# Attention in pairs of heads: scores of two pairs in one group, exponentials a beat late, two key buffers, values loaded pair by pair

## The chip, the cores and the metric

The kernel runs on one NeuronCore of a Trainium2 chip. The metric is the device time of one execution in microseconds (us), the median of several runs. Before the change it is 1545.6 us (three runs, 1545.55 to 1545.87).

Five engines work side by side, each through its own instructions in order: TensorE (PE; its weight loads appear as PEld), VectorE (DVE), ScalarE (ACT), GpSimd (POOL) and SyncE (SP), whose only work here is to issue transfers. Engines wait for one another through semaphores; what waits holds up everything behind it on its engine.

## The reference, cut to what matters

```
x = x + tanh(g_xattn) * attention(layernorm(x), ctx, mask, bias)     # 32 sequences of 64 tokens, width 512
x = x + tanh(g_ffn)   * lora_linear(layernorm(x))

def attention(hq, hkv, mask, bias):          # 32 heads of 128
    q, k, v = hq @ Wq, hkv @ Wk, hkv @ Wv
    score = q k^T / sqrt(128) + bias         # 64 x 64 for each sequence and head
    probs = where(mask, softmax(where(mask, score, -inf)), 0)
    return concat(probs @ v) @ Wo
```

Everything is float32. Most products are computed as three products of a high and a low part (a type of reduced precision, fp32r); scores and output products (probs @ v) are plain float32, which TensorE records as two passes each.

## The kernel before, in words

The 2048 tokens are worked off in two phases (`NPH`) of 1024. A phase first projects keys and values (`stage_a`) and stores them in HBM as `kd` and `vd`, then runs attention (`attention`, `run`) over 16 pairs of heads (`NPR`), and adds each pair's share of the output projection to an accumulator `acc`. The linear layer (`ffn_chunk`) follows the second phase.

The projections use seven products instead of eight for each block (`unit`, line 351): products called p1, p6, p7, p5, p2, p4, p3, in this order, each six matmuls of 512 columns. The weight of a pair is prepared by `pair_blocks` and `prep` (lines 267 to 313): four sums and seven high/low splits of 128 x 256, the high parts on ACT (L294), sums and low parts on the engine given, POOL or DVE (L287, L298). p6 needs the sums s3 and s2, in this order.

The order on each engine is that in which the Python code issues instructions (`manual_schedule`). Side work stands in generators in the list `streams`; `beat()` (line 64), called after each product, lets each of them issue one step, and `drain` issues all that is left. So the place of a step is counted in beats, of 1.36 us where a beat follows six matmuls.

For pair n the loop of `run` (lines 847 to 900) issues:

- the query unit: `unit(wq, xq)`, five of seven products, then the last two row tiles of the output projection of pair n-2 (`oproj`, L839 by way of `mm3`, L97), then the last two products (`end`);
- `pv(n-1)` (L812): 16 output products of 128 x 128 (L818, result `po`), copied to `ch` (ACT, L821) and its rest `cl` (DVE, L822);
- `scores(n, i)` for i = 0, 1 (L755): each 16 matmuls of 64 x 64, two at a time in halves of the array (L760, `ps`), then scale and bias (DVE, L762), row maximum (DVE, L764), subtraction (POOL, L765), exponential (ACT, L766);
- transfers: the next keys into one buffer `kB` (`load_k`, L702), the bias of the next pair into `sm`, and on even pairs the values of two pairs, 2 MB in two transfers (`load_v`, L706);
- six row tiles of `oproj(n-1)`. Beside them `softmax` (L769) issues by beats: sums and reciprocals (DVE), scaling (POOL), the turn `tp` (DVE), and 16 copies of 32 x 256 into `pt` (ACT, L793).

Pair 0 has a form of its own (`alone`): half of the turned probabilities are written by DVE in small transposes. The weight of pair 1 is prepared by DVE, that of pair 2 and later by POOL. At the end of a phase `last` does `finish` (two tiles of oproj(14)), other work (a half of the next phase's first key projection, or the first quarter of the linear layer), `attend` (`pv(15)`), and oproj(15).

Transfers go through SP's queue in order; each uses one of eight semaphores in turn, so a transfer is issued when the one eight places before it has landed.

Of the kernel before, what the change touches and what calls it, by code (L numbers as in the profile page):

```python
# [17 lines left out]
P = 128  # L18
# [25 lines left out]
def flamingo_block(ctx: ExitStack, tc: tile.TileContext, x, ctxT, bias, mask, gx, gf,  # L44
# [24 lines left out]
    def drain(g):  # L69
        if g in streams:  # L70
            streams.remove(g)
            for _ in g:
                pass
# [625 lines left out]
    def attention(p, res, rest):  # L699
        b = {}  # L700

        def load_k(n):  # L702
            b["k", n] = big(res[1], [P, 2, TP], F32, f"kB{p}_{n}")
            nc.sync.dma_start(out=b["k", n], in_=kd[p][n])

        def load_v(q):  # L706
            b["v", q] = [big(res[2 + c], [P, 4, 512], F32, f"v{p}_{q}_{c}") for c in range(2)]
            for c in range(2):
                nc.sync.dma_start(out=b["v", q][c], in_=vd[p][q][:, c * 4:(c + 1) * 4, :])
# [5 lines left out]
        def bias_mask(n):  # L715
            yield
            yield
            for i in range(2):
                yield
                t = sm[n % 2][:, i]  # L720
                nc.gpsimd.tensor_tensor(t, t, masks[p][0], ALU.add)  # L721

# [5 lines left out]
        def enter():  # L728
            nonlocal pt, sm
            if not sm:  # L730
                sm = [rwp.tile([P, 2, NT, S], F32, tag=f"r{2 + i}", name=f"sm{p}_{i}") for i in range(2)]
                load_bias(0)
                return bias_add
            if not pt:
                pt = big(res[0], [P, 2, NT, P], F32, f"pt{p}")
                nc.vector.memset(pt, 0.0)
                return
            fetch("q", p * NPR + 1, "r0")
            load_k(0)
            load_v(0)  # L740
# [14 lines left out]
        def scores(n, i, qT, kT):  # L755
# [9 lines left out]
            nc.gpsimd.tensor_tensor(s, s, mx.unsqueeze(2).to_broadcast([P, NT, S]), ALU.subtract)  # L765
            nc.scalar.activation(s, s, AF.Exp)  # L766
            beat()

        def softmax(n, pace):  # L769
            ss = [sm[n % 2][:, i] for i in range(2)]  # L770
            alone = pace is None
            tp = []

            def turn(i):
                tp.append(rows.tile([P, NT, S], F32, tag="row", name=f"tp{p}_{n}_{i}"))
                nc.vector.transpose(tp[i].rearrange("p a b -> p (a b)"), ss[i].rearrange("p a b -> p (a b)"))  # L776

            for i in range(2):
                nm = f"{p}_{n}_{i}"
                r = st.tile([P, NT], F32, tag="r", name=f"r{nm}")  # L780
                nc.vector.tensor_reduce(r, ss[i], AX.X, ALU.add)
                nc.vector.reciprocal(r, r)
                nc.vector.tensor_tensor(r, r, masks[p][1], ALU.mult)  # L783
                nc.gpsimd.tensor_tensor(ss[i], ss[i], r.unsqueeze(2).to_broadcast([P, NT, S]), ALU.mult)  # L784
                if alone and i:
                    turn(0)
                yield
            quads = [(h, qi, ki) for h in range(2) for qi in range(2) for ki in range(2)]

            def copy(f, i, of, h, qi, ki):  # L790
                src = slice(h * 64 + qi * 32, h * 64 + qi * 32 + 32)
                dst = slice(h * 64 + ki * 32, h * 64 + ki * 32 + 32)
                f(pt[dst, i, :, src], of[src, :, ki * 32:(ki + 1) * 32])  # L793

            if alone:
                for k, q in enumerate(quads):
                    copy(nc.scalar.copy, 0, tp[0], *q)
                    copy(nc.vector.transpose, 1, ss[1], *q)
                    if k % 3 == 2:
                        yield  # L800
                return
            for i in range(2):
                turn(i)
                yield
            todo = [(i, q) for i in range(2) for q in quads]
            for k in pace:
                for i, q in todo[:k]:
                    copy(nc.scalar.copy, i, tp[i], *q)
# [3 lines left out]
        def pv(n):  # L812

            for i, c in [(0, 0), (0, 1), (1, 0), (1, 1)] if n == 0 else [(0, 0), (1, 0), (0, 1), (1, 1)]:
                ps = psum(f"po{p}_{n}_{i}_{c}")
                hg = (2 * n + i) % 4
                for t in range(4):
                    nc.tensor.matmul(ps[:, t * P:(t + 1) * P], b["v", n // 2][c][:, t, hg * P:(hg + 1) * P],  # L818
                                     pt[:, i, c * 4 + t, :], start=True, stop=True)
                sl = slice(c * 512, (c + 1) * 512)  # L820
                nc.scalar.copy(ch[:, i, sl], ps)  # L821
                nc.vector.tensor_tensor(cl[:, i, sl], ps, ch[:, i, sl].bitcast(F32), ALU.subtract)  # L822
                beat()

        def prep_o(n):
            raw = raw_of.pop(("o", p * NPR + n))
            t = big(res[4], [P, 2, 1024], F32R, f"wo{p}_{n}")
# [8 lines left out]
        def oproj(n, t):  # L836
            w = b["o", n]
            ps = psum(f"pa{p}_{n}_{t}")
            sl = slice(t * P, (t + 1) * P)  # L839
            mm3(ps, [((ch[:, i, sl], cl[:, i, sl]), (w[:, 0, i * 512:(i + 1) * 512], w[:, 1, i * 512:(i + 1) * 512]))  # L840
                     for i in range(2)])
            nc.vector.tensor_tensor(acc[t], ps, acc[t], ALU.add)  # L842
            if n == NPR - 1 and p < NPH - 1:
                nc.sync.dma_start(out=x1d[t * P:(t + 1) * P, :], in_=acc[t])
            beat()

        def run(xq, prefetch, before_last, last_unit, last, between=None):
            soft = None
            for n in range(NPR):
                g = p * NPR + n  # L850
                qT = kqp.tile([P, 2, TP], F32, tag="kq", name=f"qT{g}")
                if n == 0:
                    qb = prep("q", g + 1, nc.vector, 2)
                    streams.append(qb)
                else:
                    streams.append(bias_mask(n))
                end = unit(wt[("q", g)], xq, None, k_dst(qT), f"q{g}", tuple(carry))
                carry.clear()
                if n == NPR - 1:
                    last_unit()  # L860
                if n == 1:
                    drain(qb)
                    fetch("q", g + 1, "r0")
                if n > 1:
                    oproj(n - 2, NT - 2)
                    oproj(n - 2, NT - 1)
                if n:
                    ob = prep_o(n - 1)
                    streams.append(ob)
                end()  # L870
                if n == 0:
                    enter_late()
                else:
                    drain(soft)
                if 0 < n < NPR - 1:
                    qb = prep("q", g + 1, nc.gpsimd, 2, 4)
                    streams.append(qb)
                if n:
                    pv(n - 1)
                    drain(ob)  # L880
                for i in range(2):
                    scores(n, i, qT, b["k", n])
                if n + 1 < NPR:
                    load_k(n + 1)
                    load_bias(n + 1)
                    if n % 2 == 0 and n:
                        load_v(n // 2)
                soft = softmax(n, None if n == 0 else (1, 2, 2, 3, 2, 2, 2, 2) if n < NPR - 1 or between else (4,) * 4)
                streams.append(soft)
                if n:  # L890
                    for t in range(NT - 2):
                        oproj(n - 1, t)
                        if n == NPR - 1 and between:
                            between(t)
                    drain(qb)
                    if n + 2 < NPR:
                        fetch("q", g + 2, "r0")
                    elif n + 2 == NPR:
                        before_last()
                if n == NPR - 5:  # L900
                    prefetch()
            ob = prep_o(n)

            def finish():
                oproj(n - 1, NT - 2)
                oproj(n - 1, NT - 1)
                streams.append(ob)

            def attend():
                drain(soft)  # L910
                drain(ob)
                pv(n)
            last(finish, attend, lambda t: oproj(n, t), acc)
# [7 lines left out]
    def frow(nm):  # L921
        rk[0] += 1
        return rwp.tile([P, 512], F32, tag=f"r{1 + rk[0] % 3}", name=nm)
# [115 lines left out]
    for p in range(NPH):  # L1039
# [4 lines left out]
        if p < NPH - 1:  # L1044
# [15 lines left out]
            def last(finish, attend, o, acc):  # L1060
                nonlocal more, kt0
                g = (p + 1) * NPR
                finish()
                fetch("k", g + 1, "r1")
# [4 lines left out]
                attend()  # L1069
# [5 lines left out]
            run(xq, prefetch, before_last, last_unit, last)  # L1075
        else:
# [11 lines left out]
            def last(finish, attend, o, acc):  # L1088
# [18 lines left out]
                finish()  # L1107
                drain(weights)
                ffn_chunk(0, first=False)
                attend()  # L1110
# [9 lines left out]
            run(xq, ffn_fetch, ffn_rows, last_unit, last, between)  # L1120
# [44 lines left out]
```

## Time and profile before

| what | value |
|---|---|
| median of the runs | 1545.6 us |
| profiled execution, its own time | 1545.82 us |
| its span, first to last instruction | 1543.8 us |
| TensorE busy | 1535.5 us (99%) |
| weight loads, VectorE, ScalarE, GpSimd busy | 1292.2, 948.3, 730.8, 1015.8 us |
| chain that ended last, share of TensorE | 95% |
| mean granted TensorE clock | 1.000 |

Lines of the profile read as follows. A group names line, engine, operation, output<-inputs, shapes and count, then the busy time in us, the mean length of one in ns, and the idle time of the engine before them with what ended it. The chain follows the work that ended last backwards; listed in order of time it gives start, length, and what. A timeline row gives start, length and count of merged instructions.

### The profile page before, as it was taken

To read this page: it belongs to the slowest core of one execution; us is meant where nothing else is said; L and a number is where in the kernel's file an instruction comes from. 1 tells how busy PE (TensorE), PEld (TensorE's weight loads), DVE (VectorE), ACT (ScalarE), POOL (GpSimd) and SP (SyncE) were. 2 spreads that over 40 slices of the span, in tenths; PEclk is the share of its full clock that TensorE was granted. 3 is DMA by queue.
4 is the path that set the end of the run, shared out by engine and by line. 5 is a ranking of instruction groups with operands and counts; after the bars stand their busy time and mean duration, and the time that the engine had idled before them with its cause. 6 is when DMAs were issued, how large, how long until landed. Compare 5 with 4: busy or idle time off the path is not lost.

```text
span 1543.8 us, 24975 instructions
## 1 busy us (share of the span) xinstructions
PE 1535.5 (99%) x9064; PEld 1292.2 (84%) x9064; DVE 948.3 (61%) x1579; ACT 730.8 (47%) x1610; POOL 1015.8 (66%) x1128
## 2 busy tenths in 40 slices
PE   9999999999999999999999999999999999999999
PEld 7888888888888888888888888888888888888887
DVE  5665343377676757575686535437767675757774
ACT  6454233345555555556445423334555555555621
POOL 3898378967665757575589837896766575757410
PEclk9999999999999999999999999999999999999999
DMA  5654444374243424531565544437424342444211
GB/s 207 243 191 177 165 171 164 137 280 177 83 177 136 163 87 177 190 141 67 213 222 191 178 170 166 164 136 282 176 83 178 137 158 94 174 189 147 80 42 69
DMA packets 80989, 246.37 MB, mean 160 GB/s; under 512 B 9857, under 2 KB 10881, under 8 KB 72674
## 3 DMA queue, kind: packets, MB, share of 16 engines
q1 hardware_dynamic: 80578, 244.26, 43.6%
q8 instruction: 71, 1.16, 0.3%
q10 hardware_dynamic: 288, 0.52, 0.1%
q14 instruction: 52, 0.43, 0.1%
HBM read 171.35 MB, written 73.40 MB: 159 GB/s over the span
## 4 chain that ended last, share of the span: by engine, by line
PE 95%; DMA 2%; DVE 2%; POOL 0%; issue 0%; ACT 0%; SPq 0%; DVEq 0%; POOLq 0%; ACTq 0%
PE pa L97 22%; PE po L818 7%; PE pzv L97 6%; PE pvv L97 6%; PE pxv L97 6%; PE pxq L97 5%; PE pzq L97 5%; PE pxk L97 5%; PE pzk L97 5%; PE pvk L97 5%; PE pvq L97 5%; PE ps L760 4%; PE ppk L97 3%; PE pyv L97 3%; PE pf L97 3%; PE pyk L97 2%
## 5 line engine op out<-in xcount | busy, mean ns | idle before, releaser
L97 PE MATMUL pa<-wo,ch 128*128 128x512 f32 x1024 | 319.9, 393 | 0.0
L793 ACT COPY pt<-tp 32x256 f32<-32x256 f32 x496 | 200.3, 404 | 87.7 <-DVE tp L776 76.6
L89 POOL TENSOR_TENSOR wo<-rawo,wo 128x512 fp32r<-128x512 f32 x64 | 81.1, 1286 | 223.3 <-ACT wo L88 215.5
L97 PEld LDWEIGHTS pa<-wo,ch 128*128 128x128 f32 x1024 | 189.4, 188 | 40.0
L842 DVE TENSOR_TENSOR acc<-pa,acc 128x512 f32<-128x512 f32 x256 | 170.0, 673 | 79.4 <-PE pa L97 79.3
L97 PE MATMUL pa<-wo,cl 128*128 128x512 f32 x512 | 199.7, 390 | 0.0
L818 PEld LDWEIGHTS po<-pt,v 128*128 128x128 f32 x1024 | 119.1, 192 | 2.6 <-ACT pt L793 0.2
L822 DVE TENSOR_TENSOR cl<-po,ch 128x512 fp32r<-128x512 f32 x128 | 88.3, 692 | 52.5 <-ACT ch L821 52.0
L818 PE MATMUL po<-pt,v 128*128 128x128 f32 x1024 | 119.4, 275 | 0.0
L97 PEld LDWEIGHTS pa<-wo,cl 128*128 128x128 f32 x512 | 96.1, 188 | 20.7
L353 DVE TENSOR_TENSOR vt<-pvv,vt 128x512 f32<-128x512 f32 x64 | 44.1, 690 | 111.9 <-PE pvv L97 111.9
L821 ACT CAST ch<-po 128x512 fp32r<-128x512 f32 x128 | 74.8, 586 | 71.5 <-PE po L818 70.9
L766 ACT ACTIVATE sm<-sm 128x512 f32<-128x512 f32 x64 | 40.6, 634 | 123.2 <-POOL sm L765 123.2
L765 POOL TENSOR_TENSOR sm<-sm,mx 128x512 f32<-128x512 f32 x64 | 66.9, 1048 | 46.8 <-DVE mx L764 46.8
L375 ACT COPY vt<-pxv 128x512 f32<-128x512 f32 x32 | 18.8, 588 | 132.1 <-PE pxv L97 132.1
L353 DVE TENSOR_TENSOR kT<-pvk,kT 128x512 f32<-128x512 f32 x56 | 38.5, 688 | 67.1 <-PE pvk L97 66.7
L721 POOL TENSOR_TENSOR sm<-sm,madd 128x512 f32<-128x512 f32 x60 | 76.3, 1292 | 2.6 <-DMA sm<-bias 2.6
L784 POOL TENSOR_TENSOR sm<-sm,r 128x512 f32<-128x512 f32 x64 | 66.8, 1044 | 14.5 <-DVE r L783 11.1
L353 DVE TENSOR_TENSOR qT<-pzq,qT 128x512 f32<-128x512 f32 x64 | 44.3, 692 | 38.0 <-PE pzq L97 37.4
L760 PE MATMUL ps<-kB,qT 128*64 128x64 f32 x2048 | 67.2, 224 | 0.3 <-DVE qT L353 0.3
L353 DVE TENSOR_TENSOR vt<-pzv,vt 128x512 f32<-128x512 f32 x64 | 44.2, 691 | 37.1 <-PE pzv L97 36.9
L760 PEld LDWEIGHTS ps<-kB,qT 128*64 128x64 f32 x2048 | 62.5, 138 | 4.9 <-issue 0.7
(978 smaller groups left out, 3704.0 us busy)
## 6 DMA issues: line engine op xcount, KB each, us to landing
kd<-kT SPq DMA_DIRECT2D x64, 512.0 KB, 3.6
vd<-vt SPq DMA_DIRECT2D x128, 256.0 KB, 2.3
kB<-kd SPq DMA_DIRECT2D x32, 1024.0 KB, 4.9
v<-vd SPq DMA_DIRECT2D x32, 1024.0 KB, 8.7
rawq<-wq SPq DMA_DIRECT2D x32, 512.0 KB, 4.0
sm<-bias SPq DMA_DIRECT2D x64, 256.0 KB, 5.3
rawo<-wo SPq DMA_DIRECT2D x32, 512.0 KB, 3.4
rawk<-wk SPq DMA_DIRECT2D x31, 512.0 KB, 5.4
```

The costliest lines, as they stand in the source:

```text
L89: eng.tensor_tensor(lo, raw, hi.bitcast(F32), ALU.subtract)
L97: nc.tensor.matmul(ps, a, b, start=start and i == 0, stop=stop and i == 3 * n - 1, skip_group_check=True)
L353: nc.vector.tensor_tensor(o, ps, i, ALU.add)
L721: nc.gpsimd.tensor_tensor(t, t, masks[p][0], ALU.add)
L760: nc.tensor.matmul(ps[h * S:(h + 1) * S, t, :], qT[:, i, tok], kT[:, i, tok], start=True, stop=True)
L765: nc.gpsimd.tensor_tensor(s, s, mx.unsqueeze(2).to_broadcast([P, NT, S]), ALU.subtract)
L784: nc.gpsimd.tensor_tensor(ss[i], ss[i], r.unsqueeze(2).to_broadcast([P, NT, S]), ALU.mult)
L793: f(pt[dst, i, :, src], of[src, :, ki * 32:(ki + 1) * 32])
L818: nc.tensor.matmul(ps[:, t * P:(t + 1) * P], b["v", n // 2][c][:, t, hg * P:(hg + 1) * P], pt[:, i, c * 4 + t, :], start=True, stop=True)
L821: nc.scalar.copy(ch[:, i, sl], ps)
L822: nc.vector.tensor_tensor(cl[:, i, sl], ps, ch[:, i, sl].bitcast(F32), ALU.subtract)
L842: nc.vector.tensor_tensor(acc[t], ps, acc[t], ALU.add)
```

## The change

It changes the order within `attention` and some of its buffers:

- `load_k` has two buffers (`res[1]`, `res[2]`); keys of pairs n+2 are loaded after the scores of n.
- `load_v` loads the values of one pair, 1 MB in rows of 1 KB, into `res[3]`, after the output products of the pair before.
- the exponential is a stream of its own (`exped`) that is added after the beat, so that it is issued at the next one.
- `softmax` is split into `normed` (sums and scaling) and `turned` (turn and copies). The form for pair 0 alone is gone. The bias of pair n+2 is loaded once pair n is turned, and its mask is added some beats later.
- the query unit is no longer interrupted by two tiles of `oproj`, and `oproj` runs eight tiles at once.
- scores are computed for pair 0 alone, then for (1, 2), (3, 4) to (13, 14), then 15. In a round of the loop, for odd a: oproj(a-3), unit(a), pv(a-2), unit(a+1), oproj(a-2), pv(a-1), scores(a), scores(a+1).
- at the start of a phase: unit(0), scores(0), unit(1), unit(2), pv(0), scores(1, 2). The weight of pair 2 is prepared by POOL during unit(1), from its fourth beat on.
- at the end: oproj(12), unit(15), pv(13), scores(15), oproj(13), pv(14), the other work (`fill`), oproj(14) with the two halves of pv(15) in it, oproj(15).
- at the start of a phase `enter` issues q1, k0, bias 1, k1, v0, where it issued q1, k0 and the 2 MB of values before; k2 and q2 follow scores(0), where k1, bias 1 and q2 did.

```diff
         def load_k(n):
-            b["k", n] = big(res[1], [P, 2, TP], F32, f"kB{p}_{n}")
+            b["k", n] = big(res[1 + n % 2], [P, 2, TP], F32, f"kB{p}_{n}")
...
-        def load_v(q):
-            b["v", q] = [big(res[2 + c], [P, 4, 512], F32, f"v{p}_{q}_{c}") for c in range(2)]
-            for c in range(2):
-                nc.sync.dma_start(out=b["v", q][c], in_=vd[p][q][:, c * 4:(c + 1) * 4, :])
+        def load_v(n):
+            b["v", n] = big(res[3], [P, NT, 256], F32, f"v{p}_{n}")
+            nc.sync.dma_start(out=b["v", n], in_=vd[p][n // 2][:, :, n % 2 * 256:(n % 2 + 1) * 256])
...
             load_k(0)
+            load_bias(1)
+            load_k(1)
             load_v(0)
...
-            nc.scalar.activation(s, s, AF.Exp)
             beat()
+            streams.append(exped(s))
+
+        def exped(s):
+            nc.scalar.activation(s, s, AF.Exp)
+            yield
...
+            def q_unit(n):
+                g = p * NPR + n
+                drain(qb.get(n))
+                if n == 0:
+                    start_q(1, nc.vector, 2)
+                elif n == 1:
+                    fetch("q", g + 1, "r0")
+                    start_q(2, nc.gpsimd, 3)
...
+            q_unit(0)
+            enter_late()
+            start_o(0)
+            b["m", 1] = bias_mask(1)
+            score(0)
+            streams.append(b["m", 1])
+            q_unit(1)
+            q_unit(2)
+            pv(0)
+            score(1, 2)
+            for a in range(3, NPR - 1, 2):
+                drain(qb[a])
+                fetch("q", p * NPR + a + 1, "r0")
+                oproj(a - 3)
+                q_unit(a)
+                start_o(a - 2)
+                pv(a - 2)
+                q_unit(a + 1)
+                oproj(a - 2)
+                start_o(a - 1)
+                pv(a - 1)
+                score(a, a + 1)
...
+            n = NPR - 1
+            oproj(n - 3)
+            q_unit(n)
+            start_o(n - 2)
+            pv(n - 2)
+            score(n)
+            oproj(n - 2, beside=between)
+            start_o(n - 1)
+            pv(n - 1)
+            fill()
+            drain(ob[n - 1])
+            start_o(n)
+            oproj(n - 1, range(4))
+            pv(n, (0,))
+            oproj(n - 1, range(4, NT))
+            pv(n, (1,))
+            last(lambda t: oproj(n, range(t, t + 1)), acc)
```

## The prediction

> **What bounds the kernel now.** I read the busy shares first, then the chain that ended last.
>
> ```profile
> PE 1535.5 (99%) x9064; PEld 1292.2 (84%) x9064; DVE 948.3 (61%) x1579; ACT 730.8 (47%) x1610; POOL 1015.8 (66%) x1128
> ...
> PE 95%; DMA 2%; DVE 2%; POOL 0%; issue 0%; ACT 0%; SPq 0%; DVEq 0%; POOLq 0%; ACTq 0%
> ...
> L97 PEld LDWEIGHTS pa<-wo,ch 128*128 128x128 f32 x1024 | 189.4, 188 | 40.0
> ```
>
> TensorE sets the time. [...] First the chain in one pair of heads (start, length, what), and where output products were followed directly by `pa` (end of phase 1):
>
> ```profile
> 577.04 3.57 PE po L818 x32
> 580.62 2.02 PE ps L760 x64
> 582.63 8.41 PE pa L97 x36
> 591.04 1.36 PE pxq L97 x6
> ...
> 597.84 2.72 PE pa L97 x12
> ```
>
> ```profile
> 730.37 3.57 PE po L818 x32
> 733.94 2.28 PE pa L97 x10
> ```
>
> The pieces touch: from 577.04 on nothing waits, and the pair repeats in 26.24 us (603.28 less 577.04). 36 `pa` after scores take 8.41 where 36 x 0.2267 is 8.16: leaving scores costs 0.25. After `po`, 10 take 2.28, next to nothing more. Inside the scores, a timeline row of 41 spans 1.39 us, each 0.22 long, so the step is (1.39-0.22)/40 = 29 ns and 64 steps 1.87; the group takes 2.02, so entering costs about 0.14. A group of scores thus costs 0.38-0.39 in turns; I use 0.38.
>
> ```profile
> 580.83 1.39 PE L760 MATMUL ps<-kB,qT 128*64 128x64 f32 x41
> ```
>
> The waits of TensorE within a phase all lie in the query unit of pair 1:
>
> ```profile
> 335.27 1.52 PE L97 MATMUL pxq<-x0p,wq1p 128*128 128x512 f32 x6
> 337.22 1.67 PE L97 MATMUL pvq<-x0p,wq1p 128*128 128x512 f32 x6 [0.42 <-DVE qT L353]
> 339.29 1.67 PE L97 MATMUL pzq<-x0p,wq1p 128*128 128x512 f32 x6 [0.40 <-DVE qT L353]
> 340.81 3.73 PE L818 MATMUL po<-pt,v 128*128 128x128 f32 x32
> ```
>
> From 335.27 to 340.81 are 5.54 us for three products of 1.36: 1.4 us lost, and as much in phase 2 (1068.05 to 1073.57).
>
> **The change, part by part.**
>
> *Scores in groups.* A phase has 9 groups of scores instead of 16, so 14 fewer in all: 14 x 0.38 = -5.3 us.
>
> *Pair 0.* The eight small DVE transposes, behind which the adds of pair 1's unit stood, are gone; DVE now has two turns of 0.69 there. -1.4 in each phase, -2.8.
>
> *Pair 2's query weight.* This decides. Before, unit(1) was followed by `pv(0)`, scores and six `oproj` tiles before unit(2). Now unit(2) follows unit(1) at once, and its weight q2 is fetched after scores(0) and k2, and prepared on POOL from the fourth beat of unit(1). Where does q2 land? In phase 2 of the profile, and the busy share of the transfer engines in phase 1 (seventh figure of a row, before GB/s):
>
> ```profile
> L263 SPq DMA_DIRECT2D rawq<-wq x1: 328/328/328, 1065.1 to 1065.1; - x1
> L294 ACT CAST wq18p<-rawq x1: 410/410/410, 1075.1 to 1075.1; 128x256 fp32r<-128x256 f32 x1
> ...
> DMA to landing us min/median/max: 7.7/7.7/7.7
> ```
>
> ```profile
> 316.00:320.00 4.00, 4.00 (x20) 3.30 (x19) 1.45 (x3) 3.24 (x7) 3.54 (x3) 1.00 0.99 416
> ...
> 332.00:336.00 4.00, 4.00 (x20) 3.30 (x19) 2.74 (x8) 1.30 (x3) 2.09 (x2) 1.00 1.02 407
> ```
>
> It lands at 1072.8, because the transfer engines are full from 312 to 338 in phase 1, and likewise in phase 2. In phase 1 the second bias (issued 331.1, 8.2 to landing) lands at 339.3; q2, 512 KB behind it at some 400 GB/s, 1.3 later: 340.6. The new order has the same bytes ahead of q2: 1 MB of k2 is added and 1 MB of the values comes later. [...] So 340.6 and 1072.8 hold. The unit(1) that doesn't wait starts at 329.70 and ends 9.65 later: 339.35, in phase 2 1072.12.
>
> POOL then issues, in order: s3, a bias mask, s2, low part of p1, a mask, s1, low p7, s4, low p6. A 128x256 step starts 0.70 after the last (579.09, 579.78, 580.46 in POOL's timeline), a mask takes 1.25 (two in 2.54). Low p6 is ready 7 x 0.70 + 2 x 1.25 = 7.4 us after landing, with 0.1 for the signal 7.5. TensorE needs it for the third matmul of the second product, 1.36 + 0.45 = 1.81 after unit(1): loss 340.6+7.5-339.35-1.81 = 6.9 in phase 1, 1072.8+7.5-1072.12-1.81 = 6.4 in phase 2. Later low parts come every 0.70 and are in time. A restart after a wait shows 1.67 for 1.52 above; three restarts in each phase, at 0.11, make 0.7. Sum +14.0. Queued behind q2's first cast on ACT: a copy of unit(1) and the first copies to `pt`, needed only at pv(0), a unit later; behind s3 on POOL: the masks, needed after pv(0).
>
> The waits would be some 1.8, 2.5 and 2.7 us long. [...] The trace shows granted clock 1.00 throughout, but no wait of this length. [...]
>
> *Steady pairs.* From scores to `pv(a)` were 8.16+9.52+2.72 us, now 10.88+9.52, with a score group of 2 us before it. Steps of `softmax` start one beat later than before and their last copies follow the sixth beat of the unit at about 26.9 after pv(a-1) began; pv(a) starts at 28.0. The before kernel had 3 us there (last copy 600.2, pv 603.28). DVE has four scores of 1.32 in a row, 2.6 us behind; eight result banks cover it. Weight preparation of even pairs fits in the 13 us of unit(a) and pv(a-2), 11 POOL steps of 0.70 and two masks. The late exponential is hidden by the 20 us before `pv`; keys and values have 13 us or more to land (4.9, 8.7 in the list of transfers; the keys now come as 2 MB), the bias some 5 before its mask (5.3 there, behind 1 MB of keys; now alone). I cost these at nothing; if the cover is gone, `pv(a)` waits.
>
> *End of the phases.* Phase 2: the weights of the linear layer are issued four beats later, so their casts (0.57 each) mix with those of `ch`; the first layer norm reaches DVE behind `cl`, two turns and a score at about 9.7 after pv(13) begins, needed by the transposes at 8.5: 1.2. Copies of pair 14 stand behind both exponentials: 0.6 before pv(14). DVE is some 4 us behind at `fill`, so the low-rank result is late by 1.2 and the next norm by 0.7. Against this, 1.4 of waits (a row at 1460.85 shows 1.04 idle) go: +2.3, bounds 0 to +5. Phase 1: pv(15) comes 10.9 after pv(14) with 16 copies of 0.404 and four other ACT steps before it: +0.3.
>
> Sum: -5.3 -2.8 +14.0 +2.6 = +8.5. The profiled execution took 1545.82 (span 1543.8, 2.0 around it); it is 0.2 above the median, so its sum carries over: 1545.6 + 8.5 = **1554.1 us**.
>
> **Rivals.** *The weight is early enough (faster).* If low p6 of pair 2 were ready by 341.2, unit(2) would not wait, and -5.3-2.8+2.6 gives 1540.1. For: it is one place in 730 us. Against: even if q2 landed at once, POOL reaches s3 only after the second scaling, at about 337.2, and 7.5 more is 344.7. It decides from a cut of the wait by four fifths; an early landing without an earlier POOL leaves 3.5 a phase and gives 1548.
> *Steady pairs wait.* If ACT's copies come 1.5 us later than worked out, pv(a) and half the others wait 0.5 to 1 us in 14 places: +7 to +14, 1561 to 1568. For: ACT's casts for the next weight stand between the copies and wait for POOL. Against: 1.1 us of slack, and 2.0 for the second block.
> [...]
> *The grouping wins nothing*, as the array would turn within the group: then 1559.4. Against: two halves of a group before (i = 0, 1) follow each other at 29 ns.
>
> **How the numbers follow.** Forecast 0.62 (1550 to 1559); early weight in part 0.10 (1547 to 1550), wholly 0.07 (about 1540); steady pairs 0.13; half clock or no gain from grouping 0.08. The range 1546 to 1564 leaves out the faster case and the upper half of the steady case. 0.2% is 3.1 us, about what a measurement can tell: faster 0.07; same (to 1548.7) 0.08; slower 0.85.
>
> **What would show it.** Right: in unit(2) of both phases (`wq2p`, `wq18p`) PE waits for POOL L298 by 6 to 7 us in total, unit(1) doesn't wait, two pairs repeat in 52.1 us instead of 52.48, 64 more scores in a group without a turn. Wrong: unit(2) starts without a wait, `po` waits for ACT `pt` in the steady rounds, or the gap before `pa` stays at one for each pair.

## The result: 1.4% slower, and outside the forecast range

The changed kernel takes 1567.24 us (median of four runs, 1565.29 to 1567.95) against 1545.61 us before (four runs, 1545.55 to 1545.87). The ratio is 1.0137, interval 1.0122 to 1.0153. The forecast was 1554.1, range 1546 to 1564. The sign was right; the size was 13 us short. The profiled execution of the changed kernel took 1565.29, with a span of 1563.5 against 1543.8: 19.8 us of the loss can be followed in the two traces. The other runs were some 2 us longer than the profiled one; the last section comes back to that.

The page of the changed kernel, first the busy shares and the chain that ended last by engine:

```profile
PE 1536.8 (98%) x9064; PEld 1293.5 (83%) x9064; DVE 937.8 (60%) x1565; ACT 740.6 (47%) x1626; POOL 1013.9 (65%) x1128
...
PE 88%; DMA 6%; POOL 3%; ACT 1%; issue 1%; DVE 1%; SPq 0%; DVEq 0%; POOLq 0%; ACTq 0%
```

TensorE has the same 9064 matmuls and is as busy as before (1536.8 against 1535.5), but only 88% of the chain runs through it, against 95%: transfers and POOL now lie on the path. (POOL now also stands 124.9 us for the bias, where it was 2.6 before; the steady rounds below show that TensorE waits for none of it there.)

A steady round, in the chain in order of time (start, length, what):

```profile
437.64 3.57 PE po L818 x32
441.21 1.38 PE pxq L97 x6
...
450.74 10.88 PE pa L97 x48
461.62 3.57 PE po L818 x32
465.19 3.88 PE ps L761 x128
469.07 11.13 PE pa L97 x48
```

The scores of two pairs now take 3.88 in one group, where two groups took 2.02 each, and there is one return to `pa` instead of two. The pieces touch, so nothing waits. The table below is made from the starts of TensorE's rows (the first product of each query unit, the first product of phase 2, the first transpose of the linear layer). It shows where the 19.8 us are. The numbers in brackets are the same stretch in the last kernel of the experiments, which hardly waits there.

| stretch (us) | before | after |
|---|---|---|
| two steady pairs (unit 10 to unit 12) | 52.47 | 52.09 |
| phase 1: unit(1) to unit(3), waits and clock | 51.31 | 46.35 (38.4) |
| phase 1: unit(13) to unit(14) | 26.23 | 16.34 (13.01) |
| phase 1: unit(15) to phase 2's first product | 28.96 | 32.17 (29.72) |
| phase 2: unit(1) to unit(3) | 51.30 | 46.44 (38.5) |
| phase 2: unit(13) to unit(14) | 26.23 | 14.63 (13.01) |

All rows but the first hold other work than before, since products moved across their edges (the fourth has 64 `po` and 48 `pa` where it had 32 and 60). So they are read against the number in brackets, which has the same work; 13.01 is also what a steady round takes.

**The start of a phase.** TensorE's timeline of the changed kernel; what ended the idle time stands in the square brackets.

```profile
337.81 1.52 PE L97 MATMUL pzq<-x0p,wq1p 128*128 128x512 f32 x6
340.67 0.73 PE L97 MATMUL pxq<-x0p,wq2p 128*128 128x512 f32 x2 [1.33 <-ACT wq2p L294]
343.69 1.30 PE L97 MATMUL pxq<-x0p,wq2p 128*128 128x512 f32 x4 [2.29 <-POOL wq2p L298]
344.78 1.05 PE L97 MATMUL pyq<-x0p,wq2p 128*128 128x512 f32 x2
347.66 2.07 PE L97 MATMUL pyq<-x0p,wq2p 128*128 128x512 f32 x4 [1.82 <-POOL wq2p L298]
349.53 2.44 PE L97 MATMUL pvq<-x0p,wq2p 128*128 128x512 f32 x6
```

These are the three waits that the forecast named, for the casts and the low parts of q2. But the product at 349.53 takes 2.44 us, not 1.52. The view by stretches shows why (after each window its length, then busy time and number of rows of PE, PEld, DVE, ACT and POOL, then the granted clock, the share of the transfer engines and GB/s):

```profile
337.81:341.22 3.41, 2.08 (x9) 1.24 (x7) 1.98 (x3) 1.01 (x3) 0.90 (x2) 1.00 0.90 346
341.22:344.63 3.41, 1.12 (x5) 0.81 (x5) 0.00 (x0) 1.78 (x5) 3.41 (x4) 1.00 0.04 17
344.63:348.05 3.42, 1.60 (x5) 0.78 (x4) 0.00 (x0) 2.05 (x6) 3.42 (x6) 0.50 0.00 0
348.05:351.46 3.41, 3.41 (x9) 2.64 (x9) 0.69 (x1) 3.22 (x9) 3.41 (x5) 0.50 0.21 64
351.46:354.87 3.41, 3.41 (x16) 2.78 (x16) 1.38 (x2) 0.47 (x2) 2.86 (x4) 1.00 0.24 93
```

For 6.83 us, two stretches of 3.41, the clock is at half, and in the second one TensorE doesn't wait: 9 matmuls are done where the next stretch does 16. Phase 2 has the same from 1088.74 on.

**The round with the prefetch.** The copies to `pt` of pair 13 come late. TensorE's and ACT's timelines of the changed kernel:

```profile
645.82 1.05 PE L818 MATMUL po<-pt,v 128*128 128x128 f32 x8
649.94 2.95 PE L818 MATMUL po<-pt,v 128*128 128x128 f32 x24 [3.07 <-ACT pt L804]
```

```profile
638.47 1.25 ACT L804 COPY pt<-tp 32x256 f32<-32x256 f32 x3
643.87 0.41 ACT L294 CAST wq14p<-rawq 128x256 fp32r<-128x256 f32 x1 [4.14 <-DMA rawq<-wq]
644.18 0.83 ACT L804 COPY pt<-tp 32x256 f32<-32x256 f32 x2
```

ACT stands 4.14 us at the first cast of q14, whose raw weight has not landed, with the last eight copies to `pt` of pair 13 behind it in its queue. TensorE waits 3.07 us for them at the second block of `pv(13)`. In phase 2 it waits 1.36 in the same place (the row at 1392.11), and the stretch is 1.6 longer.

Why the weight is late is read from SP's timeline, first of the kernel before (the weight there is q13), then of the changed kernel; `c` is the prefetch.

```profile
616.48 0.33 SPq L263 DMA_DIRECT2D rawq<-wq  x1
616.86 4.17 SPq L411 DMA_DIRECT2D c<-ctxT  x8
```

```profile
626.01 11.55 SPq L411 DMA_DIRECT2D c<-ctxT  x8
637.91 0.33 SPq L263 DMA_DIRECT2D rawq<-wq  x1
```

Before, the weight went ahead of the eight loads of the prefetch. Now they are ahead of it; issuing them takes 11.55 us, since the last three wait until the transfers eight places before them, values and 2 MB of keys, have landed; and q14 lands 5.9 us after its own issue, at 643.84.

**The ends.** In TensorE's timeline the waits at the end of phase 1 are for `wo` (1.10) and `pt` (0.82, 0.42). At the end of phase 2 they are these, each ahead of a transpose of the linear layer, beside one of 0.64 for `wo` at 1450.95:

```profile
1453.81 0.63 PE L136 MATMUL tpf<-ident,xn 128*128 128x128 f32 x4 [0.77 <-DVE xn L131]
...
1456.80 0.63 PE L136 MATMUL tpf<-ident,xn 128*128 128x128 f32 x4 [0.97 <-DVE xn L131]
...
1475.24 0.66 PE L136 MATMUL tpf<-ident,xn 128*128 128x128 f32 x4 [0.90 <-DVE xn L131]
```

### The profile page after: what moved, and what is told of

Same layout as the page of the kernel before. It is cut to its first block, busy times and chain, and to the rows that moved or that the text cites. A ratio compares the mean times of both kernels' runs of the same rounds, so it can differ in the third digit from the quotient of the medians.

```text
span 1563.5 us, 25230 instructions
## 1 busy us (share of the span) xinstructions
PE 1536.8 (98%) x9064; PEld 1293.5 (83%) x9064; DVE 937.8 (60%) x1565; ACT 740.6 (47%) x1626; POOL 1013.9 (65%) x1128
## 4 chain that ended last, share of the span: by engine, by line
PE 88%; DMA 6%; POOL 3%; ACT 1%; issue 1%; DVE 1%; SPq 0%; DVEq 0%; POOLq 0%; ACTq 0%
PE pa L97 19%; PE po L818 7%; PE pvv L97 5%; PE pxv L97 5%; PE pzv L97 5%; PE pxk L97 5%; PE pzk L97 5%; PE pvk L97 5%; PE pvq L97 4%; PE pzq L97 4%; PE pxq L97 4%; PE ps L761 4%; PE pyv L97 3%; PE ppk L97 3%; PE pf L97 2%; PE pyk L97 2%
## 5 line engine op out<-in xcount | busy, mean ns | idle before, releaser
L804 ACT COPY pt<-tp 32x256 f32<-32x256 f32 x512 | 206.6, 403 | 62.0 <-DVE tp L793 50.0
L719 POOL TENSOR_TENSOR sm<-sm,madd 128x512 f32<-128x512 f32 x60 | 76.7, 1289 | 124.9 <-DMA sm<-bias 124.9
L353 DVE TENSOR_TENSOR qT<-pvq,qT 128x512 f32<-128x512 f32 x64 | 44.1, 689 | 74.9 <-PE pvq L97 74.9
L353 DVE TENSOR_TENSOR kT<-pvk,kT 128x512 f32<-128x512 f32 x56 | 38.5, 688 | 67.4 <-PE pvk L97 66.8
L191 POOL TENSOR_TENSOR vs<-wvr,wvr 128x512 f32<-128x512 f32 x24 | 30.8, 1294 | 54.4 <-DMA wvr<-wv 54.4
```

The source lines that it names most:

```text
L353: nc.vector.tensor_tensor(o, ps, i, ALU.add)
L804: nc.scalar.copy(pt[dst, i, :, src], tp[i][src, :, ki * 32:(ki + 1) * 32])
```

## The experiments

They are told in the order in which they were made. Each edit is shown, cut to what matters, against the kernel that the text below it starts from. "Median" is of all its runs; stretches are those of the table.

### Useless matmuls in the waits

```diff
     def unit(...):
+        f0, f1, f2 = (5, 10, 9) if nm in ("q2", f"q{NPR + 2}") else (0, 0, 0)
...
-        product(px, "p1", w, a, sl, True)
+        product(px, "p1", w, a, sl, True, f0, f1)
...
-        product(py, "p6", w, a, sl, True)
+        product(py, "p6", w, a, sl, True, 0, f2)
...
+                nc.tensor.matmul(idle[0][:, :P], ident, ident, start=True, stop=True)
```

> The changed kernel, with 5, 10 and 9 matmuls without use (128x128, about 0.23 us each) put where unit(2) waits in each phase: ahead of its first product, ahead of the third matmul of that product, and ahead of the third matmul of its second product. They are shorter in sum than the waits (1.5, 2.5 and 2.1 us in the profile), so by themselves they cost nothing. Theory (TensorE standing still makes the clock fall to half for 6.8 us): the granted clock stays at 1.00 through both starts, and 3.3 us in each phase come back: about 6.5 us less than the changed kernel (about 1559 to 1561). Rival (the clock falls for another reason, the load or the sequence before): clock 0.5 again for 6.8 us behind the waits, and the time within 1 us of the changed kernel's.

Median 1561.5 us, ratio to before 1.0104 (1.0089 to 1.0119), span 1558.7. The same stretches as above:

```profile
337.81:341.22 3.41, 3.25 (x20) 2.73 (x19) 2.79 (x5) 0.60 (x2) 1.27 (x2) 1.00 0.97 369
341.22:344.63 3.41, 3.36 (x24) 3.02 (x25) 0.00 (x0) 2.18 (x6) 3.41 (x5) 1.00 0.17 64
344.63:348.05 3.42, 3.13 (x23) 2.73 (x21) 0.00 (x0) 1.67 (x6) 3.42 (x6) 1.00 0.03 5
```

The weights come no earlier, yet the clock stays at 1.00 in both phases of the profile: it was TensorE's standing still that halved it. What this is worth is read from unit(2) to unit(3): 35.20 to 33.43 us in phase 1, 35.37 to 33.44 in phase 2, so 3.7 us in all. I had expected 6.5; most of the first of the two stretches at half clock falls on time in which TensorE waits anyway. The span fell by 4.8; beyond these 3.7, the rounds with the prefetch took 1.3 less, which this edit doesn't touch, and I did not follow that.

### q2 fetched early and prepared on DVE

```diff
         def enter_late():
...
             fetch("o", p * NPR, "r1")
-            for t in range(NT):
-                nc.sync.dma_start(out=acc[t], in_=x[p * NT + t])
...
                 elif n == 1:
                     fetch("q", g + 1, "r0")
-                    start_q(2, nc.gpsimd, 3)
+                    load_k(2)
+                    load_acc()
+                    start_q(2, nc.vector, 3)
```

> The changed kernel, with the fetch of q2 put ahead of the second key load and of the eight loads of acc (3 MB less ahead of it), and q2 prepared on DVE instead of POOL, so that the two bias masks no longer stand between its steps. Theory (the start costs about 6 us of waits and 3.3 us of half clock in each phase, and the weight is the only reason): unit(2) waits for less than 1 us, the clock stays at 1.00, and 18 to 20 us are gone: 1547 to 1549. Rival (DVE is itself full there: 1.9 of 2 us busy from 334 to 338): the low parts come late from DVE, 2 to 3 us of waits a phase stay, with or without half clock: 1552 to 1558. A third: acc lands too late for the first output products, and what is won at unit(2) is paid at oproj(0).

Median 1553.9, ratio 1.0052 (1.0035 to 1.0069), span 1551.1. q2 lands at 332.29 instead of 340.19. The rival was the better forecast: DVE's low parts leave waits of 1.2 and 0.9 us in each phase, but the clock stays at 1.00. Unit(1) to unit(3) falls from 46.35 to 40.42 and from 46.44 to 40.41, 12.0 us together. No wait of TensorE for `acc` appeared. So some 60% of the loss lay at q2.

### The prefetch behind q14

```diff
             for a in range(3, NPR - 1, 2):
                 drain(qb[a])
                 fetch("q", p * NPR + a + 1, "r0")
+                if a == NPR - 3:
+                    prefetch()
                 oproj(a - 3)
...
                 score(a, a + 1)
-                if a == NPR - 5:
-                    prefetch()
```

> The changed kernel, with the eight loads of prefetch() issued behind the fetch of q14 (top of the next round) instead of ahead of it; nothing else is moved. Theory (the 3.2 us before pv(13) in phase 1 and 1.5 us in phase 2 come from q14, which lands behind 2 MB of keys and 2 MB of prefetch; its cast holds the copies to pt up in ACT's queue): q14 lands some 5 us earlier, pv(13) waits for nothing in both phases, 4.7 us less than the changed kernel: about 1561 to 1562. Rival (the casts of q14 wait for POOL or the copies are late for another reason, as in a round with less slack): pv(13) waits as before, and the time is within 1 us of the changed kernel's.

Median 1561.92, ratio 1.0102 (1.0087 to 1.0117). Unit(13) to unit(14) falls from 16.34 to 13.40 and from 14.63 to 13.01: 4.6 us, as expected. In ACT's timeline of this kernel the first cast of q14 waits for nothing:

```profile
637.97 0.41 ACT L294 CAST wq14p<-rawq 128x256 fp32r<-128x256 f32 x1
```

The order in SP's queue comes from the program: before, the round of pair 11 ended with the fetch of q13 and then `prefetch()`; in the changed kernel `prefetch()` ends a round and the fetch of q14 opens the next.

### The exponential at once

```diff
             nc.gpsimd.tensor_tensor(s, s, mx.unsqueeze(2).to_broadcast([P, NT, S]), ALU.subtract)
+            nc.scalar.activation(s, s, AF.Exp)
             beat()
-            streams.append(exped(s))
```

> The changed kernel, with each exponential issued at once behind its subtraction, as in the kernel before, instead of a beat late. Theory (the late exponential is hidden by some 20 us and wins or costs nothing by itself): within 2 us of the changed kernel's time. Rival (without the delay ACT stands in its queue for POOL's subtraction while the eviction copies of ch are behind it, with four groups in a row): PE waits for result banks or pv's copies after every score group, 0.3 to 1 us in each of 14 rounds, 5 to 14 us more than the changed kernel.

Median 1575.68, ratio 1.0188 (1.0169 to 1.0208): 8.4 us slower than the changed kernel. The theory was wrong; the rival's size (5 to 14 us) came true, but not its place. Steady rounds take 39.08 and 13.01 us as in the changed kernel, so nothing is paid in each round. It is paid where ACT's queue is short of time: unit(1), 11.15 to 12.57 and 11.07 to 12.56; unit(15) to phase 2's first product, 32.17 to 36.51; unit(13) to unit(14) of phase 2, 14.63 to 17.39; the end, 2.9. In the second and third of these a part is the clock, which is at half for a stretch from 725.18 and from 1397.61. In turn unit(2) to unit(3) takes 0.6 and 2.6 less, as unit(1) ends later and less of the wait for q2 is left (in phase 2 without half clock). ACT at the end of phase 1 in this kernel:

```profile
714.68 0.63 ACT L767 ACTIVATE sm<-sm 128x512 f32<-128x512 f32 x1 [5.10 <-POOL sm L766]
...
718.16 0.63 ACT L767 ACTIVATE sm<-sm 128x512 f32<-128x512 f32 x1 [1.93 <-POOL sm L766]
718.81 6.38 ACT L804 COPY pt<-tp 32x256 f32<-32x256 f32 x15
```

The exponential stands for POOL's subtraction, and fifteen copies to `pt`, 0.4 us each, stand behind it; TensorE needs them from 720.6 on.

### Early q2 on POOL, and the prefetch behind q14

```diff
-                    start_q(2, nc.gpsimd, 3)
+                    start_q(2, nc.gpsimd, 1)
```

with the moved loads and the moved prefetch of the two runs above.

> The changed kernel with the early fetch of q2 and the later prefetch of the runs before, and with q2 prepared on POOL from the second beat of unit(1) (before: from the fourth), so that its steps stand ahead of the scalings and of the masks. Theory (three separate sums: waits at the start 13.0, half clock there 3.7, round with the prefetch 4.6 to 4.9; nothing else in the steady rounds): unit(2) waits for nothing, clock 1.00, pv(13) waits for nothing, 21 us less than the changed kernel by the profiled span, 1563.5 - 21.3 = 1542 (median some 1544 to 1546). What is then left above the sum of the gains (5.3 + 2.8) lies at the ends of the phases. Rival (POOL's other work, taken further back, makes pv(0) or the first rounds late): 2 us or more of new waits behind unit(2).

Median 1552.23, ratio 1.0041 (1.0026 to 1.0056), span 1551.3 where 1542 was expected. TensorE waits once in each unit(2), for 2.3 us, ahead of the third matmul of p6, and then the clock is at half for one stretch: with both, unit(2) to unit(3) takes 3.6 us more than the 28.8 of the last kernel below. `pv(13)` of phase 1 still waits 0.67. POOL's timeline of this kernel:

```profile
335.52 1.04 POOL L787 TENSOR_TENSOR sm<-sm,r 128x512 f32<-128x512 f32 x1 [0.17 <-DVE r L786]
336.52 0.73 POOL L287 TENSOR_TENSOR wsq<-rawq 128x256 f32<-128x256 f32 x1
337.42 1.04 POOL L787 TENSOR_TENSOR sm<-sm,r 128x512 f32<-128x512 f32 x1 [0.17 <-DVE r L786]
...
341.20 1.28 POOL L719 TENSOR_TENSOR sm<-sm,madd 128x512 f32<-128x512 f32 x1
...
343.11 0.73 POOL L298 TENSOR_TENSOR wq2p<-wsq,wq2p 128x256 fp32r<-128x256 f32 x1
```

The weight is there from 333.2, but scalings, a mask and the steps of p7 stand ahead of the low part of p6 (343.11). An early transfer alone does not move an engine that is booked.

### The same, with two moves at the ends

```diff
+                if n == NPR - 1:
+                    last_unit()
                 end()
...
-                if n == NPR - 1:
-                    last_unit()
...
             oproj(n - 3)
-            q_unit(n)
             start_o(n - 2)
+            q_unit(n)
```

> The kernel of start_and_prefetch, with two moves at the end of each phase: the preparation of wo13 is issued ahead of the last query unit instead of behind it, and the stream of last_unit (first blocks of phase 2, weights of the linear layer) begins behind the fifth product of that unit, as in the kernel before, instead of behind the seventh. Theory (the ends cost 3.4 us in phase 1 and 3.0 in phase 2 because wo13 and the layer norms are issued too late in their queues): the waits for POOL wo (1.27 and 0.8) and for DVE xn (0.93, 1.14, 1.14) go or shrink, 3 to 5 us less than start_and_prefetch. Rival (ACT and DVE are simply full there: the work is late whatever the order): the waits move to pt and ch, less than 1.5 us won.

Median 1547.72, ratio 1.0015 (1.0006 to 1.0023), span 1545.7. Unit(15) to phase 2's first product falls from 32.16 to 29.72, the stretch from unit(15) of phase 2 to the first transpose from 19.89 to 18.08, and what follows takes 0.4 longer: 3.8 us won by order alone. The waits for `wo` and the first two for `xn` are gone. `pv(13)`, though, waits again (1.37 and 0.54), and its two stretches take 1.3 more. What more than makes up for this is the clock, and it teaches something. This kernel waits in unit(2) for as long, but has no stretch at half clock:

```profile
339.80:343.21 3.41, 2.07 (x9) 1.22 (x7) 0.97 (x2) 2.81 (x8) 3.41 (x5) 1.00 1.03 394
343.21:346.62 3.41, 2.43 (x11) 2.01 (x12) 0.69 (x1) 2.97 (x7) 3.41 (x5) 1.00 0.17 63
```

and this is the run before it, without the moves at the ends:

```profile
340.73:344.14 3.41, 1.09 (x5) 0.62 (x4) 0.00 (x0) 3.00 (x8) 3.41 (x5) 1.00 0.77 300
344.14:347.55 3.41, 3.41 (x9) 2.63 (x9) 0.69 (x1) 3.22 (x9) 3.41 (x5) 0.50 0.01 2
```

The wait of 2.3 us is the same in both. It falls into one stretch there (TensorE busy for 1.09 of 3.41) and is parted over two here (2.07 and 2.43). The stretch from unit(2) to unit(3) takes 32.35 there and 30.84 here.

### The score groups parted again

```diff
...
                 start_o(a - 1)
+                score(a)
                 pv(a - 1)
-                score(a, a + 1)
+                score(a + 1)
```

> The kernel of start_and_prefetch, with the scores of pair a ahead of pv(a-1) instead of beside those of pair a+1: 12 groups of scores more in all, with the same matmuls, copies, keys and exponentials. Theory (a group of scores costs 0.38 us in turns, and nothing else is won by the grouping): two pairs repeat in 52.5 us instead of 52.1, 12 x 0.38 = 4.6 us more than start_and_prefetch. Rival (the turn is paid elsewhere, so grouping wins nothing): the same time; another (the softmax of pair a, begun earlier, disturbs the copies of pair a-1): more than 7 us more, with waits for pt.

Median 1554.4, ratio 1.0058 (1.0041 to 1.0075), 2.2 us above the unparted kernel. The spans differ by 0.7 only, because this profile has one stretch at half clock less (1.7 us) and its rounds with the prefetch take 1.1 less; the steady rounds tell it without these. In the chain of this kernel:

```profile
446.68 10.88 PE pa L97 x48
457.56 2.02 PE ps L763 x64
459.57 3.77 PE po L820 x32
463.34 2.02 PE ps L763 x64
465.36 11.11 PE pa L97 x48
```

Scores take 4.04 instead of 3.88, and `po` after scores takes 3.77 instead of 3.57. Two pairs take 52.41 instead of 52.09: 0.32 for a group, a little less than the 0.38 of the forecast, as the way back from scores is cheaper to `po` (0.20) than to `pa` (0.25). For 12 groups that is 3.8 us.

### One part alone in the kernel before: the late exponential

```diff
             nc.gpsimd.tensor_tensor(s, s, mx.unsqueeze(2).to_broadcast([P, NT, S]), ALU.subtract)
-            nc.scalar.activation(s, s, AF.Exp)
             beat()
+            streams.append(exped(s))
```

> The kernel before, with one part of the change alone: each exponential is issued one beat behind its subtraction. Theory (with single groups of scores ACT has time to wait for POOL's subtraction, so the delay wins nothing by itself, and its cost is hidden): 1545.6 within 1 us. Rival (the waits in unit(1), 1.4 us in each phase, came from the exponentials standing in ACT's queue ahead of the copies): 2 to 3 us less, 1543.

Median 1543.92, ratio 0.9987 (0.998 to 0.9994): the rival was right, at some 1.9 us, just under its 2 to 3. Unit(1) to unit(2) falls from 25.08 to 24.27 and from 25.07 to 24.30. Of the two waits of unit(1), each some 0.4, one is gone:

```profile
337.51 1.56 PE L97 MATMUL pvq<-x0p,wq1p 128*128 128x512 f32 x6
339.38 1.65 PE L97 MATMUL pzq<-x0p,wq1p 128*128 128x512 f32 x6 [0.31 <-DVE qT L353]
```

In ACT's timeline the first copy to `qT` of unit(1) starts at 332.98, between the two exponentials, 2.41 us after the unit began (330.57); before, it stood behind both, at 333.64, 3.94 after the beginning (329.70).

### All of it, POOL's order mended too

```diff
+    PREP2 = (("s3", "hp1"), ("s2", "lp1", "hp6"), ("lp6", "hp7"), ("s1", "lp7", "hp5"), ...)
...
-                    start_q(2, nc.gpsimd, 1)
+                    start_q(2, nc.gpsimd, 0, 0, PREP2)
...
-            b["m", 1] = bias_mask(1)
+            b["m", 1] = bias_mask(1, 9)
```

and the key loads of the steady rounds behind the fetch of the next query weight.

> The kernel of start_prefetch_ends, with three more moves: POOL prepares q2 from the first beat of unit(1), with the low part of p6 ahead of that of p7; the two masks of pair 1 come five beats later; and the key loads of the steady rounds are issued behind the fetch of the query weight instead of ahead of it. Theory (the wait of 2.5 us in each phase before the third matmul of p6 is POOL's queue: two scalings and a mask ahead of the low part; and what is left before pv(13), 1.4 and 0.6, is q14 behind 2 MB of keys): both are gone, 1545.7 - 5.0 - 2.0 = 1538.7 by the span, a median of 1540 to 1542, 0.3% under the kernel before. Rival (POOL's scalings of pair 0, now behind steps that wait for q2, or the masks, become late and hold pv(0) or score(1)): a new wait of 1 to 3 us in each phase, and no less than 1544.

Median 1542.83, ratio 0.998 (0.9973 to 0.9988), span 1540.9, clock 1.00. Unit(2) waits for nothing in phase 1, and unit(2) to unit(3) takes 28.76 us (35.20 in the changed kernel). Instead `pv(0)` waits for 0.41 and 0.68. But unit(13) to unit(14) in phase 1 is still 14.64, so moving the keys was not the cure there. POOL's timeline of this kernel gives the reason:

```profile
632.48 0.73 POOL L298 TENSOR_TENSOR wq14p<-rawq,wq14p 128x256 fp32r<-128x256 f32 x1
636.50 1.28 POOL L722 TENSOR_TENSOR sm<-sm,madd 128x512 f32<-128x512 f32 x1 [3.29 <-DMA sm<-bias]
637.75 0.73 POOL L287 TENSOR_TENSOR wsq<-rawq 128x256 f32<-128x256 f32 x1
```

q14 is there (it landed at 625.10), but its next step stands behind a mask, whose bias lands behind the prefetch (its second half at 637.07).

### The prefetch behind the bias too

```diff
                 keys()
-                if a == NPR - 3:
-                    prefetch()
                 oproj(a - 3)
                 q_unit(a)
+                if a == NPR - 3:
+                    prefetch()
```

> The kernel of all_cures, with the eight loads of prefetch() issued behind the query unit of pair 13, and so behind the bias of pair 13 too. Theory (the 1.4 us that pv(13) still waits in phase 1 come from that bias: it lands behind the 2 MB of the prefetch, POOL stands at its mask for 3.3 us, the steps of q14 stand behind the mask, and ACT's cast for them holds up the copies to pt): pv(13) waits for nothing, 1.4 to 1.6 us less by the span than all_cures (1540.9), about 1539.4. Rival (the prefetch, 11 us later, is late for what reads it at the end of the phases): as much or more is lost behind it.

Median 1541.64 (1540.49 to 1543.2), ratio 0.9973 (0.9962 to 0.9983), the lowest median of all the kernels here, though the interval overlaps that of the run before. `pv(13)` runs in one piece, and the stretch takes 13.01 in both phases:

```profile
639.78 3.73 PE L823 MATMUL po<-pt,v 128*128 128x128 f32 x32
```

The span is 1540.7, only 0.2 less than in the run before, because in this profile the first query unit starts 1.9 us later, ahead of every edit; from there on it takes 2.1 less, of which this stretch is 1.6.

## Why the prediction was wrong in size: step by step

The same 9064 matmuls run in both kernels (TensorE busy for 1535.5 and 1536.8 us), so the forecast adds up what turns between kinds of matmuls and waits cost. The loss of 19.8 us in the spans, beside its terms:

| step | forecast | measured |
|---|---|---|
| 14 fewer groups of scores | -5.3 | -5.3 (7 x 0.38 in a phase; 52.47 to 52.09) |
| unit(1) of pair 1 no longer waits | -2.8 | -2.9 (11.1 to 9.65 in each phase) |
| pair 2's weight late | +14.0 | +13.1 |
| clock at half behind those waits | 0 | +3.7 |
| steady pairs | 0 | 0, but +4.9 in the two rounds with the prefetch |
| ends of the phases | +2.6 | about +6 |

The third row is 46.35 and 46.44, less 38.4 and 38.5 (the last kernel), less the 1.8 and 1.9 of the clock, plus the 0.40 and 0.47 that `pv(0)` waits in the last kernel. The fifth is 16.34 + 14.63 - 2 x 13.01. The last is what remains; waits of 4.6 us are seen in it (2.3 in phase 1; 3.3 in phase 2, less the 1.0 that the kernel before had there), and the rest was not taken apart. So of the 11.3 us by which the sum was short, 4.9 are the rounds with the prefetch, 3.7 the clock and some 3.7 the ends, less 1 us in the other terms. The median is short by 1.8 more, because the other three runs took longer than the profiled one.

*Scores in groups*: right. 7 x 0.38 was seen, and the groups parted again gave most of it back.

*Pair 0*: right in size, wrong in its reason. I put the waits of unit(1) down to the eight small transposes on DVE. The late exponential alone, in the kernel before, took away over half of them (0.8 of 1.4), and the exponential at once in the changed kernel, where the small transposes are gone, brought waits of 1.3 and 0.7 back. ACT's queue was the cause of at least that part; what the transposes did to the rest was not tried alone.

*Pair 2's query weight*: right in mechanism, place and size. q2 landed at 340.19 (forecast 340.6), and the three waits for the cast, the low part of p1 and the low part of p6 lie where they were put, each somewhat shorter (1.33, 2.29 and 1.82 in phase 1, where 1.8, 2.5 and 2.7 were forecast). It was the largest term, and "the weight is early enough" fell with it. The remark that an early landing without an earlier POOL leaves 3.5 us a phase came out near: with q2 early and POOL begun two beats earlier 3.6 were left, but 1.3 or more of this was half clock, which the remark did not count.

*Half clock at the waits*: this step failed. The sum has nothing for it, and the range keeps up to 3.4 us, a figure that no run shows: the kernel before has no wait of TensorE over 1.04 us and a clock of 1.000. The runs showed this in its place: no wait in unit(2) is longer than 2.29 us, and still the clock fell to half, for two stretches of 3.41 in each phase. The wait of 3.07 before `pv(13)`, the longest of all, left it at 1.00. Not the length of a wait counted here but the idle time within one stretch: after 1.12 us of work in 3.41 (1.34 in phase 2) the clock was at half, after 1.86 it was not. The cost was 3.7 in all, hardly above the 3.4 of the range.

*Steady pairs*: this step failed, and it is the one with a new cause. Ten rounds of two pairs cost nothing, as worked out (52.08 or 52.09 us each), and the rival "steady pairs wait" was wrong for them. But one round in each phase is not like the others. It carries a prefetch of 2 MB, and the change moved the fetch of the next query weight, and the next bias, from ahead of that prefetch in SP's queue to behind it. I counted bytes ahead of q2 at the start, and did not count them for the one round with other traffic. ACT's in-order queue then turned a late weight into late copies of another pair.

*Ends of the phases*: mis-sized, and most of all in phase 1, where +0.3 was forecast and waits of 2.3 came. Phase 2's mechanism was named rightly (the first two norms behind `cl`, 0.77 and 0.97 against 1.2, and the next, 0.90 against 0.7), and its waits rose by 2.2 where +2.3 was forecast. Left out in both was the wait for `wo13` (1.10 and 0.64), whose preparation used to have part of a query unit between itself and its use and now has only `pv(13)` and a group of scores. The copies of pair 14 behind both exponentials, forecast for phase 2 at 0.6, came in phase 1 at 0.82; those of pair 15 waited 0.42. The two moves at the ends won 3.8 us of this.

So the change has a gain of some 8 us that is real, and 28 us of loss from orders at the edges of the phase that had to be made anew with it. With these orders mended it is 0.27% faster than the kernel before (interval 0.17 to 0.38%). Of that margin the late exponential gives 0.13% by itself, without any grouping.

## What to carry to other kernels

Before costing a reordered loop at nothing, list the rounds that are not like the others (the first, the last two, the one that prefetches), and for each in-order queue write down what now stands ahead of what: here all the losses were there, and none in the other rounds. A transfer that is late costs whatever stands behind its first reader: here a cast that stood 4.14 us on ACT for its weight delayed copies that belong to other work, and TensorE stood 3.07 for them. Where a wait on TensorE can't be removed, matmuls without use inside it may be worth a try: here the clock stayed at 1.00 with them, and 1.8 to 1.9 us were won in each phase.

## What the runs showed of the hardware

What I had not expected is how little idle time in a stretch was followed by half clock. The granted clock changed on a step of 3.413 us: in the changed kernel the two times at half clock last 6.827 us each, two steps, and begin at 344.635 and at 1088.740 us, 218.0 steps apart; with early q2 on POOL the clock is at half for one step, from 344.14 to 347.55. In the changed kernel, leaving out the first 10 us and the stretches in which the program ends, I compared TensorE's idle time in each full-speed stretch of this length (its length less PE busy) with the clock of the next. After the two in which TensorE stood for 2.29 and 2.07 us the clock was at half; after all others, in which it stood for 1.55 or less, the clock was at 1.00. So no stretch without work was needed here. The stretches at half clock in which TensorE stood for 1.82 and 2.16 us were followed by another, those in which it stood for none by full clock: two in each phase.

So the same wait of 2.3 us cost a stretch at half clock or none by where it fell (340.73 to 344.14 against 339.80 to 346.62 above). A longer one was harmless too: the 3.07 us before `pv(13)` in the changed kernel are parted into 1.55 and 1.52.

```profile
645.01:648.42 3.41, 1.86 (x13) 1.51 (x11) 1.03 (x2) 2.68 (x7) 3.41 (x5) 1.00 0.00 0
648.42:651.83 3.41, 1.89 (x16) 1.89 (x17) 0.16 (x1) 3.23 (x9) 3.41 (x5) 1.00 0.00 0
```

That is a likely reason why the kernels with such waits spread more from run to run, though no run shows it: the changed kernel's clock was 0.993 to 0.996 in its four runs, the lowest in the three that took longest, where the last two kernels show 0.999 to 1.000. It is not the whole reason, as the kernel with the useless matmuls ranged from 1560.4 to 1565.2 at clocks of 0.998 to 1.000; what else spreads it stayed open.
